# A recurrent block with routed experts on one core: gates by exp, ln and sigmoid instead of reciprocals, an earlier first job, output weights loaded further ahead

## The chip, the core and the metric

The kernel runs on one core of one Trainium2 chip. The metric is the device time of one execution in microseconds (us), as a median over runs. PE is the matmul engine (TensorE), DVE the vector engine, ACT the scalar engine, POOL the GpSimd engine, and SP the queue that issues most DMA transfers.

## What is computed

The input is x of 8 sequences of 1024 tokens with 512 features in float32. It is normalised (xn), and then two branches run on xn.

```
# recurrent branch, 512 -> 3 x 1024 -> 1024 -> 512
hidden, forget_gate, input_gate = split(xn @ W1 + b1)
diff           = softplus(-forget_gate) - softplus(-input_gate)
log_coeffs     = -softplus(diff)        # coefficient of the old state: f/(f+i), f and i the sigmoids
log_val_coeffs = -softplus(-diff)       # coefficient of the new value: i/(f+i)
h = scan over the tokens of  coeff * h + val_coeff * g(hidden)     # done in logs in the reference
s = h @ W2 + b2
# feed-forward branch
shared = (silu(xn @ shared_gate_w) * (xn @ shared_up_w)) @ shared_down_w
e      = argmax(xn @ gate_w)            # one of 32 experts per token
routed = (silu(xs @ gate[e]) * (xs @ up[e])) @ down[e],  xs = xn * sigmoid(max logit)
out    = x + s * silu(shared + routed)
```

Here g(v) is v + 0.5 for v >= 0 and sigmoid(v) below. In the reference the gates are called f for forget and i for input. In the kernel, the tile that holds the forget branch ends as the weight of the new value, and the tile that holds the input branch ends as the coefficient of the old state: with u_f and u_i the biased projections, sigmoid of (ln(1+exp(-u_f)) - ln(1+exp(-u_i))), negated or not, gives the two.

## The kernel before

**Stages.** The 8192 tokens are worked through in 16 chunks of 512 tokens (`NCHUNK`), features on the partitions. The first chunk is prepared at the top of the kernel (statistics, normalisation, PE transposes into `xnT`), the others while the chunk ahead of them is computed. After the chunks come the dispatch of tokens to experts, and then the 32 experts with a fixed number of tokens each, and a loop for tokens that were left over.

**Slots.** The order of all instructions in the chunk stage is written out by hand. Time is counted in slots. A chunk has 20 jobs (`JC`) of 7 slots, so 140 slots (`SC`). A job is one weight block of 512 x 256 (`natural`, tiles called `nat`): kinds f, i and h of the recurrence and g and u of the shared feed-forward, each in four pairs of 128 features. `at(slot, step)` puts a step into a slot, and the main loop first emits the matmuls of the slot with their evictions, then the slot's steps, and then as many matmuls of the output projection as are `due`. Every engine works in the order in which its instructions were emitted.

**Chunk 0** uses `plain`: per job 2 blocks of 4 matmuls of 512 columns, one per slot and two in the seventh. Each block has a PSUM bank of its own from `ps_b` (three banks), and ACT evicts it, with the bias where there is one. In the same chunk `combine` forms for each job the four weight sums S (`sums`), which `save` stores to DRAM for the later chunks: S0 and S3 on POOL, S1 and S2 on DVE.

**Chunks 1 to 15** use `multiply`: a 2 x 2 block scheme with seven half-sized products P1 to P7 instead of eight, each two matmuls of 256 columns, in the order P1, P4 (of two jobs back), P5, P7 (of one job back), P2, P6, P3. P1, P6, P7 and P4 accumulate in one bank (`b`), P5 and P3 in another (`c`), P2 in `a`; between two products of a bank ACT copies what stands in it, and DVE or POOL adds the parts one slot later (`join`). P3 is 4 slots after P5, the others in a bank are 5 slots apart. The sums of the moving operand, `t_sum`, are made on DVE at slots -5, -2, 3 and 8 of the chunk.

**Gates.** `Cell` works on one pair, 128 x 1024 elements. Its slots count from the first slot of the pair's f job. Before, with m = min(f, i, 0): POOL forms m - f and m - i (`less`), ACT takes exp of m, f and i, POOL adds m to f and i (`weigh`), DVE adds f and i (`total`), takes two reciprocals of 128 x 512 (`invert`) and multiplies both by them (`divide`). ACT's sigmoid and relu of h, two DVE steps (`value`, `weighed`) and two scans end the cell. Two tiles, tags `m` and `d`, are shared by all cells, one buffer each.

**Output projection.** `project_out` multiplies the recurrence's h by W2 and the shared hidden layer by its down weights, with the same seven products in units of one chunk and one of the two halves. A product is 8 matmuls (16 in the trace), and takes one weight block of 0.5 MB (`wP`), from the weights or from sums stored in `tdram`. `out_fetch` issues the next load whenever a product ends, into three buffers. The last two units run alone after the last job, while the experts' first weights (2 MB each, `e_wg`, `e_wu`, `e_wd`) are loaded on the same SP queue.

**Dispatch.** `Dispatch.ranks`, `places` and `slots` are generators that run one step per slot near the end of the chunks. A `yield` is a pause of one slot. `places` forms `terms` on DVE, pauses, and multiplies them on PE. Then 64 `enter` steps on POOL write token numbers into tables, `collect` and `merge` join these, and the experts' tokens are gathered.

In the trace every matmul stands as two records (two passes).

Of the kernel before, what the change touches and what calls it, by code (L numbers as in the profile page):

```python
# [8 lines left out]
FP = mybir.dt.float32  # L9
I32 = mybir.dt.int32  # L10
AF = mybir.ActivationFunctionType
ALU = mybir.AluOpType
# [21 lines left out]
def tile_kernel(  # L34
# [621 lines left out]
    for n in range(NJOB):  # L656
        if n >= 3:
            at(7 * (n - 2) + 2, load, n)
        if n >= JC:
            at(7 * (n - 2) + 4, fetch, n)  # L660
        else:
            for q, s in ((0, 0), (1, 2), (2, 3), (3, 4)):
                at(7 * n + s, combine, n, q)
            at(7 * n + 10, save, n)

# [32 lines left out]
    def plain(n, s):  # L698

        kind = JOBS[n % JC][1]  # L700
        for m in (s, s + 1) if s == 6 else (s,):
            block, k = divmod(m, KH)
            if k == 0:
                banks[n, block] = ps_b.tile([P, 512], FP, tag="b", name=f"b{block}_{n}")
            ps = banks[n, block]
            nc.tensor.matmul(  # L706
                ps, lhsT=natural[n][:, k, block * P : (block + 1) * P], rhs=xnTs[0][:, k, :],
                start=(k == 0), stop=(k == KH - 1),
            )
            if k == KH - 1:  # L710
                o = outs[n] if block else out_of(n)
                if kind in "gu":
                    nc.scalar.copy(o[:, block, :], ps)
                else:
                    nc.scalar.activation(o[:, block, :], ps, AF.Identity, bias=bias(n, block))

    def multiply(name, n):

# [77 lines left out]
    class Cell:  # L796
# [8 lines left out]
        def low(self):  # L805
            n = JC * self.c + JOBS.index((self.p, "f"))
            self.f, self.i, self.h = (outs[n + q] for q in range(3))

            self.m = self.tmp("m")
            nc.vector.scalar_tensor_tensor(self.m, self.f, 0.0, self.i, ALU.min, ALU.min)  # L810

        def less(self, v):
            v = getattr(self, v)
            nc.gpsimd.tensor_tensor(v, self.m, v, ALU.subtract)  # L814

        def exp(self, v):
            v = getattr(self, v)
            nc.scalar.activation(v, v, AF.Exp)

        def weigh(self, v):  # L820

            v = getattr(self, v)
            nc.gpsimd.tensor_tensor(v, self.m, v, ALU.add)  # L823

        def total(self):
            self.d = self.tmp("d")
            nc.vector.tensor_tensor(self.d, self.i, self.f, ALU.add)

        def invert(self, s):
            nc.vector.reciprocal(self.d[:, s, :], self.d[:, s, :])  # L830

        def divide(self, v):
            v = getattr(self, v)
            nc.vector.tensor_tensor(v, v, self.d, ALU.mult)

        def sigmoid(self):
            self.e = self.tmp("m")
# [25 lines left out]
        def plan(self):  # L863
            g = SC * self.c + 7 * JOBS.index((self.p, "f"))
            for slot, what, *args in (
                (24, self.low), (25, self.less, "f"), (25, self.less, "i"),
                (27, self.exp, "m"), (29, self.exp, "f"), (31, self.exp, "i"),
                (32, self.weigh, "f"), (33, self.weigh, "i"), (37, self.total),
                (38, self.invert, 0), (39, self.sigmoid), (40, self.positive),
                (41, self.invert, 1), (43, self.value), (44, self.weighed),  # L870
                (45, self.divide, "f"), (46, self.divide, "i"),
                (47, self.scan, 0), (48, self.scan, 1),
            ):
                at(g + slot, what, *args)

# [73 lines left out]

    units = [(c, half) for c in range(NCHUNK) for half in range(2)]  # L950
    out_w, out_s = {}, {}
    out_next = iter([(u, name) for u in units for name in UNIT])

    def out_fetch():

        u, name = next(out_next, (None, None))
        if u is None:
            return
        half = u[1]
        o = out_w[u, name] = out_tile(f"w{name}_{half}")  # L960
        if name in ("P1", "P2", "P3"):
            k, m = {"P1": (0, 0), "P2": (1, 0), "P3": (1, 1)}[name]
            nc.sync.dma_start(out=o, in_=out_block(half, k, m))
        else:
            q = {"P5": 1, "P6": 2, "P7": 3, "P4": 4}[name]
            nc.sync.dma_start(out=o.rearrange("p q f -> p (q f)"), in_=tdram[half, q][:, :])
# [97 lines left out]
    class Dispatch:  # L1064
# [69 lines left out]
        def places(self):  # L1134
# [42 lines left out]
                    terms[:, q * E : (q + 1) * E], of, by[:E, 0:1], None, ALU.mult  # L1177
                )
            nc.vector.tensor_copy(terms[:, 4 * E :], extra)
            for _ in range(4):  # L1180
                yield
            ps = work("terms")
            nc.tensor.matmul(
# [136 lines left out]
    for t in range(NT):  # L1320
        first.stats(t)
        first.variance(t, 1)
        first.spread(t, 1)
        if t:
            first.normal(t - 1)
            first.transpose(t - 1)
    first.normal(NT - 1)
    first.transpose(NT - 1)
    vps = work("vps")
# [71 lines left out]
    for now in range(END):  # L1401
# [153 lines left out]
```

## Time and profile before

| | us |
|---|---|
| median of 3 runs | 4299.56 (4299.24 to 4302.12) |
| profiled execution | 4299.96 |
| its span, first to last instruction | 4298.2 |
| PE busy | 4221.4 (98%) |
| DVE busy | 2830.7 (66%) |
| POOL busy | 1751.5 (41%) |
| ACT busy | 1607.1 (37%) |
| reciprocals (L830), 128 of 3.34 us on DVE | 427.9 |
| activation table loads in the gates, 127 of 1.28 us | 162.9 |

The page gives busy time per engine over the span, the groups of instructions by line with what ended the idle time before them, and the chain that ended last. The trace answers the same for any stretch of time. A wait is written as "engine, what it was to do, its line <- engine, what released it, its line", with the total in us, how often, and the longest. L706 is a matmul of chunk 0, L746 one of `multiply`, L1033 one of the output projection; L713 and L715 are the evictions in chunk 0, L760 and L762 those of `multiply`; L810 to L856 are the steps of `Cell`; L678 is `t_sum`, L488 a transpose of the preparation, L519 the router, L1183 the matmul of `terms`.

### The profile page before, as it was taken

Reading aid. Unit: us, or ns where it says so; the run is one execution under the profiler, and the core shown is the slowest. Engines: PE = TensorE matmul, PEld = TensorE weight load, DVE = VectorE, ACT = ScalarE, POOL = GpSimd, SP = SyncE. Lnnn points to the kernel's source line nnn. Section 1 sums busy time; section 2 is a strip of 40 time slices with the busy share of each in tenths; the row PEclk is TensorE's granted clock in tenths of the full one; section 3 lists DMA queues with packets and bytes.
Section 4 is the critical chain, followed back from the end, with each engine's and each line's share of the span. In section 5 each row is a group of like instructions: output and inputs, shape, how many; then the busy total and the mean of one; then the engine's idle time right before and its main releaser. Section 6 shows DMA issues by size and latency. Waiting matters only on the chain.

```text
span 4298.2 us, 52089 instructions
## 1 busy us (share of the span) xinstructions
PE 4221.4 (98%) x18703; PEld 3534.2 (82%) x18703; DVE 2830.7 (66%) x3637; ACT 1607.1 (37%) x3193; POOL 1751.5 (41%) x1410
## 2 busy tenths in 40 slices
PE   8899999999999999999999999999999999999998
PEld 3488888888888888888888888866777788889998
DVE  6786876887878768888787698823444444544444
ACT  3355555555555555555555554501111111111110
POOL 4444444543444445434444444741333233233221
PEclk9999999999999999999999999999999999999999
DMA  7567666666666666766666664575566657677773
GB/s 247 202 217 225 203 222 206 216 220 220 210 216 207 221 209 210 225 216 210 218 211 222 209 206 152 157 263 186 205 224 234 228 205 252 219 253 247 241 266 112
DMA packets 507240, 925.63 MB, mean 215 GB/s; under 512 B 38397, under 2 KB 325021, under 8 KB 498786
## 3 DMA queue, kind: packets, MB, share of 16 engines
q1 hardware_dynamic: 479394, 832.27, 58.7%
q0 software_dynamic: 27584, 89.98, 6.3%
q8 instruction: 150, 2.46, 0.2%
q14 instruction: 112, 0.92, 0.1%
HBM read 805.27 MB, written 134.92 MB: 219 GB/s over the span
## 4 chain that ended last, share of the span: by engine, by line
PE 91%; DVE 4%; POOL 2%; issue 2%; DMA 1%; ACT 0%; SPq 0%; POOLq 0%; DVEq 0%; ACTq 0%
PE b L746 23%; PE u L1033 17%; PE c L746 11%; PE e_g L272 11%; PE e_u L272 11%; PE acc L261 11%; PE a L746 6%; DVE d L830 1%; POOL i L814 0%; PE b L706 0%; DMA wP<-tdram 0%; PE lgp L519 0%; POOL tab L1280 0%; POOL i L823 0%; POOL f L823 0%
## 5 line engine op out<-in xcount | busy, mean ns | idle before, releaser
L746 PE MATMUL b<-t,sums 128*128 128x256 f32 x2400 | 619.2, 381 | 8.5 <-DVE t L678 6.3
L1033 PE MATMUL u<-wP,s 128*128 128x256 f32 x2048 | 600.8, 380 | 2.7 <-DMA wP<-tdram 2.7
L272 PE MATMUL e_g<-e_xsT,e_wg 128*128 128x296 f32 (+15 forms) x2048 | 518.3, 396 | 1.0 <-DVE e_xsT L243 1.0
L272 PE MATMUL e_u<-e_xsT,e_wu 128*128 128x296 f32 (+15 forms) x2048 | 518.2, 396 | 0.0
L746 PEld LDWEIGHTS b<-t,sums 128*128 128x128 f32 x2400 | 455.0, 191 | 74.4 <-issue 6.5
L261 PE MATMUL acc<-e_h,e_wd 128*128 128x296 f32 (+15 forms) x2048 | 513.0, 396 | 0.0
L272 PEld LDWEIGHTS e_g<-e_xsT,e_wg 128*128 128x128 f32 x2048 | 389.7, 190 | 87.5 <-DVE e_xsT L243 1.2
L261 PEld LDWEIGHTS acc<-e_h,e_wd 128*128 128x128 f32 x2048 | 389.8, 190 | 86.3
L272 PEld LDWEIGHTS e_u<-e_xsT,e_wu 128*128 128x128 f32 x2048 | 389.8, 190 | 86.4
L277 ACT ACTIVATE e_sig<-e_g 128x280 f32<-128x280 f32 (+15 forms) x256 | 101.9, 398 | 935.5 <-PE e_g L272 930.7
L1033 PEld LDWEIGHTS u<-wP,s 128*128 128x128 f32 x2048 | 390.2, 191 | 57.0 <-issue 5.0
L279 DVE TENSOR_TENSOR e_sig<-e_sig,e_g 128x280 f32<-128x280 f32 (+15 forms) x256 | 113.2, 442 | 481.9 <-ACT e_sig L277 481.5
L830 DVE RECIPROCAL d<-d 128x512 f32<-128x512 f32 x128 | 427.9, 3344 | 1.6
L359 POOL DMA_INDIRECT out_dram<-e_rest,idx x84 | 93.4, 1112 | 804.1 <-DVE e_rest L358 801.0
L213 POOL DMA_INDIRECT e_xs<-rec,fours x276 | 262.0, 949 | 180.9 <-DMA e_rest<-rec,idx 80.9
L814 POOL TENSOR_TENSOR f<-m,f 128x1024 f32<-128x1024 f32 x64 | 154.7, 2418 | 410.6 <-DVE m L810 321.8
L746 PE MATMUL c<-t,sums 128*128 128x256 f32 x1200 | 309.2, 380 | 6.4 <-DVE t L678 6.4
L746 PE MATMUL c<-xnT,sums 128*128 128x256 f32 x1200 | 310.3, 381 | 0.3
L746 PE MATMUL a<-xnT,nat 128*128 128x256 f32 x1200 | 309.9, 381 | 0.0
L746 PE MATMUL b<-xnT,nat 128*128 128x256 f32 x1200 | 308.1, 379 | 0.0
L746 PE MATMUL b<-t,nat 128*128 128x256 f32 x1200 | 308.1, 379 | 0.0
L280 DVE TENSOR_TENSOR e_h<-e_sig,e_u 128x280 f32<-128x280 f32 (+15 forms) x256 | 113.2, 442 | 245.7 <-PE e_u L272 245.4
(241 smaller groups left out, 7370.6 us busy)
## 6 DMA issues: line engine op xcount, KB each, us to landing
sums<-sdram SPq DMA_DIRECT2D x300, 512.0 KB, 4.8
nat<-in_L_attn_W_dram SPq DMA_DIRECT2D x192, 512.0 KB, 4.4
wP<-tdram SPq DMA_DIRECT2D x128, 512.0 KB, 4.3
e_wg<-L_ffn_routed_gate_w_dram SPq DMA_DIRECT2D x32, 2048.0 KB, 8.5
e_wu<-n_L_ffn_routed_up_w_dram SPq DMA_DIRECT2D x32, 2048.0 KB, 11.6
e_wd<-L_ffn_routed_down_w_dram SPq DMA_DIRECT2D x32, 2048.0 KB, 19.3
nat<-L_ffn_shared_gate_w_dram SPq DMA_DIRECT2D x64, 512.0 KB, 4.6
nat<-n_L_ffn_shared_up_w_dram SPq DMA_DIRECT2D x64, 512.0 KB, 4.3
```

The source lines that it names most:

```text
L213: nc.gpsimd.indirect_dma_start(out=r[:, b, :], out_offset=None, in_=rec1.rearrange("n (a d) -> (n a) d", a=NA), in_offset=bass.IndirectOff ...
L261: nc.tensor.matmul(accs[m][:, :W], lhsT=wd[:, j, m * P : (m + 1) * P], rhs=h[:, :W], start=(j == 0), stop=(j == NI - 1),)
L272: nc.tensor.matmul(o[:, :W], lhsT=w[:, k, j * P : (j + 1) * P], rhs=xsT[:, k, :W], start=(k == 0), stop=(k == KH - 1),)
L277: nc.scalar.activation(sig[:, :W], g[:, :W], AF.Sigmoid)
L279: nc.vector.tensor_tensor(sig[:, :W], sig[:, :W], g[:, :W], ALU.mult)
L280: nc.vector.tensor_tensor(h[:, :W], sig[:, :W], u[:, :W], ALU.mult)
L359: nc.gpsimd.indirect_dma_start(out=of[:, :], out_offset=bass.IndirectOffsetOnAxis(ap=col[:n, :], axis=0), in_=z, in_offset=None, bounds_ch ...
L746: nc.tensor.matmul(ps, lhsT=lhs[:, k, :], rhs=rhs[:, k, :], start=(new and k == 0), stop=(k == KQ - 1),  skip_group_check=True,)
L814: nc.gpsimd.tensor_tensor(v, self.m, v, ALU.subtract)
L830: nc.vector.reciprocal(self.d[:, s, :], self.d[:, s, :])
L1033: nc.tensor.matmul(ps[:, q, :], lhsT=lhs[:, q * P : (q + 1) * P], rhs=w[:, p, :],  start=(q == 0 and p == 0 and name in ("P1", "P2", "P5") ...
```

## The change

- The gates are computed as sigmoid of d and of -d, where d is ln(1+exp(-|f|)) - min(f,0) less the same of i, up to its sign. ACT does Abs, Exp and Ln of f and of i and the two sigmoids; DVE does `difference`, `less` and `more`. POOL does nothing in the cell. The scans stand at slots 45 and 47 instead of 47 and 48.
- The first job's matmuls are split into two halves of 256 tokens. The first half is emitted after the transposes of tiles 0 and 1, ahead of those of tiles 2 and 3 (`first_half`).
- `combine` of the sums S stands at slots 0, 2, 4 and 7 of a job (in the order S0, S2, S1, S3) instead of 0, 2, 3 and 4 (S0, S1, S2, S3).
- After the last job two more buffers (`far`) are made for output weights and two loads are issued at once, ahead of the first expert's weights; from there on two of five loads go to `far`.
- `places` pauses 9 slots instead of 4 between `terms` and its matmul.

```diff
-            for q, s in ((0, 0), (1, 2), (2, 3), (3, 4)):
+            for q, s in ((0, 0), (2, 2), (1, 4), (3, 7)):
                 at(7 * n + s, combine, n, q)
...
-            if k == 0:
+            if k == 0 and n:
                 banks[n, block] = ps_b.tile([P, 512], FP, tag="b", name=f"b{block}_{n}")
             ps = banks[n, block]
+            part = slice(0 if n else HT, T)
             nc.tensor.matmul(
-                ps, lhsT=natural[n][:, k, block * P : (block + 1) * P], rhs=xnTs[0][:, k, :],
-                start=(k == 0), stop=(k == KH - 1),
+                ps[:, part], lhsT=natural[n][:, k, block * P : (block + 1) * P],
+                rhs=xnTs[0][:, k, part], start=(k == 0), stop=(k == KH - 1),
             )
...
+    def first_half():
+        for block in range(2):
+            ps = banks[0, block] = ps_b.tile([P, 512], FP, tag="b", name=f"b{block}_0")
+            for k in range(KH):
+                nc.tensor.matmul(
+                    ps[:, :HT], lhsT=natural[0][:, k, block * P : (block + 1) * P],
+                    rhs=xnTs[0][:, k, :HT], start=(k == 0), stop=(k == KH - 1),
+                )
...
-            self.m = self.tmp("m")
-            nc.vector.scalar_tensor_tensor(self.m, self.f, 0.0, self.i, ALU.min, ALU.min)
...
-            nc.gpsimd.tensor_tensor(v, self.m, v, ALU.subtract)
+            t = self.tmp(tag)
+            setattr(self, "l" + v, t)
+            nc.scalar.activation(t, getattr(self, v), AF.Abs)
...
-            nc.scalar.activation(v, v, AF.Exp)
...
-            nc.gpsimd.tensor_tensor(v, self.m, v, ALU.add)
...
-            nc.vector.tensor_tensor(self.d, self.i, self.f, ALU.add)
...
-            nc.vector.reciprocal(self.d[:, s, :], self.d[:, s, :])
...
-            nc.vector.tensor_tensor(v, v, self.d, ALU.mult)
+            nc.scalar.activation(v, v, AF.Exp, scale=-1.0)
...
+            nc.scalar.activation(v, v, AF.Ln, bias=ones[:, 0:1])
...
+            nc.vector.tensor_tensor(d, d, self.li, ALU.subtract)
...
+            nc.vector.scalar_tensor_tensor(d, self.i, 0.0, d, ALU.min, ALU.add)
...
+            nc.vector.scalar_tensor_tensor(d, self.f, 0.0, d, ALU.min, ALU.subtract)
...
+            nc.scalar.activation(getattr(self, v), self.d, AF.Sigmoid, scale=sign)
...
-                (24, self.low), (25, self.less, "f"), (25, self.less, "i"),
-                (27, self.exp, "m"), (29, self.exp, "f"), (31, self.exp, "i"),
-                (32, self.weigh, "f"), (33, self.weigh, "i"), (37, self.total),
-                (38, self.invert, 0), (39, self.sigmoid), (40, self.positive),
-                (41, self.invert, 1), (43, self.value), (44, self.weighed),
-                (45, self.divide, "f"), (46, self.divide, "i"),
-                (47, self.scan, 0), (48, self.scan, 1),
+                (24, self.size, "f", "d"), (25, self.exp, "lf"), (26, self.size, "i", "m"),
+                (28, self.exp, "li"), (29, self.log, "lf"), (31, self.log, "li"),
+                (32, self.difference), (33, self.less), (34, self.more),
+                (36, self.gate, "i", 1.0), (37, self.gate, "f", -1.0),
+                (39, self.sigmoid), (40, self.positive),
+                (42, self.value), (43, self.weighed), (45, self.scan, 0), (47, self.scan, 1),
...
-        o = out_w[u, name] = out_tile(f"w{name}_{half}")
+        if "far" in pools:
+            turn = next(far_turn)
+            if turn % 5 < 2:
+                o = pools["far"].tile([P, NP, HC], FP, tag="far", name=f"far{turn}")
+            else:
+                o = out_tile(f"w{name}_{half}")
+            out_w[u, name] = o
+        else:
+            o = out_w[u, name] = out_tile(f"w{name}_{half}")
...
-            for _ in range(4):
+            for _ in range(9):
                 yield
...
+        if t == 2:
+            first_half()
...
+    pools["far"] = c1.enter_context(tc.tile_pool(name="far", bufs=2, side="right"))
+    for _ in range(2):
+        out_fetch()
     chunks[0].weight("g")
```

More of the change, by code (lines that the diff above doesn't have):

```diff
@@ L803, in tmp, with size, log, difference @@
             return jp.tile([P, 2, T], FP, tag=tag, name=f"{tag}{self.c}_{self.p}", bufs=1)
-        def low(self):
+        def size(self, v, tag):
             n = JC * self.c + JOBS.index((self.p, "f"))
             self.f, self.i, self.h = (outs[n + q] for q in range(3))
-            self.m = self.tmp("m")
-            nc.vector.scalar_tensor_tensor(self.m, self.f, 0.0, self.i, ALU.min, ALU.min)
-        def less(self, v):
-            v = getattr(self, v)
-            nc.gpsimd.tensor_tensor(v, self.m, v, ALU.subtract)
+            t = self.tmp(tag)
+            setattr(self, "l" + v, t)
+            nc.scalar.activation(t, getattr(self, v), AF.Abs)
         def exp(self, v):
             v = getattr(self, v)
-            nc.scalar.activation(v, v, AF.Exp)
-        def weigh(self, v):
+            nc.scalar.activation(v, v, AF.Exp, scale=-1.0)
+        def log(self, v):
             v = getattr(self, v)
-            nc.gpsimd.tensor_tensor(v, self.m, v, ALU.add)
-        def total(self):
-            self.d = self.tmp("d")
-            nc.vector.tensor_tensor(self.d, self.i, self.f, ALU.add)
[L829 to L833, printed above, removed]
-            nc.vector.tensor_tensor(v, v, self.d, ALU.mult)
+            nc.scalar.activation(v, v, AF.Ln, bias=ones[:, 0:1])
+        def difference(self):
+            self.d = d = self.lf
+            nc.vector.tensor_tensor(d, d, self.li, ALU.subtract)
+        def less(self):
+            d = self.d
+            nc.vector.scalar_tensor_tensor(d, self.i, 0.0, d, ALU.min, ALU.add)
+        def more(self):
+            d = self.d
+            nc.vector.scalar_tensor_tensor(d, self.f, 0.0, d, ALU.min, ALU.subtract)
+        def gate(self, v, sign):
+            nc.scalar.activation(getattr(self, v), self.d, AF.Sigmoid, scale=sign)
         def sigmoid(self):
@@ L951, in tile_kernel @@
     out_w, out_s = {}, {}
+    far_turn = iter(range(2 * len(UNIT)))
     out_next = iter([(u, name) for u in units for name in UNIT])
```

## The prediction

> **What bounds the kernel now.** I read the busy shares first, then busy time by stage, then what PE waited for, then ACT's and DVE's timelines at those waits.
>
> ```profile
> PE 4221.4 (98%) x18703; PEld 3534.2 (82%) x18703; DVE 2830.7 (66%) x3637; ACT 1607.1 (37%) x3193; POOL 1751.5 (41%) x1410
> ```
>
> PE is idle for only 4298.2 - 4221.4 = 76.8 us. The change removes no matmul, so I need to know where these 76.8 us lie. By stage (the stretch in us, its length, then busy time and count of PE, PEld, DVE, ACT and POOL, PE's granted clock, DMA share, GB/s):
>
> ```profile
> 12.90:180.20 167.30, 151.42 (x349) 65.59 (x348) 120.44 (x171) 58.84 (x75) 88.60 (x69) 0.95 0.66 224
> 180.20:204.00 23.80, 14.87 (x57) 12.11 (x57) 21.82 (x30) 6.68 (x14) 4.23 (x4) 0.86 0.41 139
> 204.00:2440.00 2236.00, 2235.28 (x10379) 1949.56 (x10378) 1746.12 (x1909) 1201.73 (x2397) 1002.51 (x715) 1.00 0.67 216
> 2440.00:2660.00 220.00, 209.69 (x953) 180.98 (x952) 175.50 (x236) 107.33 (x216) 99.22 (x72) 0.98 0.58 183
> 2800.00:2850.00 50.00, 41.12 (x183) 34.93 (x183) 14.53 (x25) 4.68 (x8) 19.49 (x21) 0.97 0.89 310
> 2850.00:4277.80 1427.80, 1427.25 (x6144) 1168.52 (x6143) 620.10 (x1132) 151.47 (x340) 426.58 (x435) 1.00 0.65 224
> ```
>
> From 204 to 2440 us PE misses 0.7 us: the 13 chunks there cannot get faster, though most of the reciprocals run in them. The expert stage from 2850 on is full and untouched. What can be won lies in chunk 0 and its end, around the dispatch table, and at the hand-over to the experts. PE's waits name the causes (total us, times, longest):
>
> ```profile
> PE b L706 <- ACT u L713: 10.7, 2, 5.7
> PE terms L1183 <- DVE terms L1179: 6.5, 1, 6.5
> PE c L746 <- DVE t L678: 6.4, 1, 6.4
> PE b L746 <- DVE t L678: 6.3, 3, 3.8
> PE u L1033 <- DMA wP<-L_ffn_shared_down_w_dram: 5.2, 1, 5.2
> PE lgp L519 <- DVE xnT L488: 3.7, 1, 3.7
> PE u L1033 <- DMA wP<-tdram: 2.7, 1, 2.7
> ```
>
> The first is an ACT eviction queued behind a gate exp that waits for POOL; the third is `t_sum` queued behind reciprocals (timelines of ACT and DVE: start, duration, operation, idle time before it):
>
> ```profile
> 78.58 1.06 ACT L818 ACTIVATE m<-m 128x1024 f32<-128x1024 f32 x1 [5.29 <-POOL i L814]
> 80.49 0.56 ACT L713 COPY u<-b 128x512 f32<-128x512 f32 x1
> ...
> 177.00 6.55 DVE L830 RECIPROCAL d<-d 128x512 f32<-128x512 f32 x2
> ...
> 185.89 0.68 DVE L678 TENSOR_TENSOR t<-xnT 128x512 f32<-128x512 f32 x1
> ```
>
> After each long wait the matmuls also run slow for some us. PE's timeline, with one pass of 512 columns at 0.427 us and of 256 at 0.215 us when full: 40 passes took 19.69 instead of 17.1 from 81.11, 50 took 24.37 instead of 21.35 from 124.72, 14 took 7.97 instead of 6.0 from 153.76, 12 took 5.8 instead of 2.6 from 186.62; small rest 0.4: **11 us** in chunk 0 and its end. Likewise 2.5 us after the wait at 2575, 1.7 at 2620, 1.9 at 2816.
>
> **What the Trainium skill says.** "TensorE: Matmul & The Clock Gate", What's actually happening: the clock halves after an idle window of about 3.4 us and returns after as long busy. The trace agrees (waits of 3.7 us and more are followed by slow passes; that of 1.59 us at 2702 is not). "ScalarE: Activation LUTs", What ACT_TABLE_LOAD costs: 1283 ns and a drain of about 1380 ns. The trace has 1283 ns, but no drain: a load ends at 852.44 and its exp starts at 852.45. I use 1.28. "SBUF — State Buffer", the shared port pair of DVE and POOL: a two-input DVE operation and a POOL one exclude each other; it fits L847, 1.22 us alone and 1.75 beside POOL.
>
> **The change, part by part.**
>
> *Gates, 64 cells.* Removed from DVE: L810 1.22, L827 1.26, two reciprocals 6.69, two L834 3.04 = 12.2; added: three at 1.22 = 3.7; saves 8.5 per cell. POOL loses 2.42 + 2.73 + 2.41 + 2.45 = 10.0 per cell. An Abs, an Ln and a scaled Exp or Sigmoid stand in no row; I price them at the rows of Exp, Sigmoid and Relu, 1.05 to 1.06 us (the same ScalarE section gives every function one rate), low end the same, high end 1.2 with the bias pointer of Ln. ACT gets eight activations for three and one more table load (the built kernel's ACT list has a load before exp, before ln and before sigmoid; Abs needs none): 5 x 1.06 + 1.28 = +6.6 us per cell; its share in the full chunks goes from 1202/2236 = 54% to about 69%. ACT gate work waits for POOL no more; the one cross-engine wait is gate i behind three DVE steps.
>
> Does PE feel ACT? The tightest use is P5 (slot phase 2) to P3 (phase 6, same bank): P5's eviction must end before P3's slot. A slot is 170.7/140 = 1.22 us (784 passes x 0.215 and the router). Back to back an activation costs 0.96 us and an eviction 0.36. From slot 24 (time 0): Abs, eviction, load and Exp, eviction, Abs end at 6.06; eviction, eviction, Exp 7.72; eviction, load, Ln 10.33; P5's eviction of slot 30 ends at 10.69, P3 of slot 34 starts at 12.2: **1.5 us spare**. The second Ln ends at 12.0; on DVE difference, less and more with 1 to 2.5 us of queued joins and preparation end at 16.7 to 18.2; gate i ends at 18.1 to 19.3, P5's eviction of slot 37 at 19.6 at worst, P3 of slot 41 starts at 20.7: **1.1 us spare**. An output eviction (0.58) fits into either. What queues on DVE behind `difference` are joins, whose parts have two buffers, and `t_sum`, 7 slots ahead. The kernel before already shows such lags without loss:
>
> ```profile
> 940.62 1.06 ACT L818 ACTIVATE m<-m 128x1024 f32<-128x1024 f32 x1 [3.20 <-POOL i L814]
> 941.59 0.35 ACT L760 COPY p<-b 128x256 f32<-128x256 f32 x1
> ```
>
> So I charge 3 us for new ACT waits; from 0 to 25 (0.4 per cell in 60 cells).
>
> *Chunk 0.* Idle 5.71 + 1.51 + 4.98 + 3.68 + 6.42 + 0.51 + 2.00 = 24.8, slow 11: 36 us. Every one of these waits has reciprocals or POOL's subtractions ahead of it. DVE needs 120 us of 167 there and loses some 30; POOL loses 40. ACT's burst there lags 3 to 4 us, its three 512-wide banks allow two blocks, 6.9 us. I take 33 back (20 to 36).
>
> *Sums S spread out.* Same four operations per job, 20 jobs. It breaks up POOL and DVE waiting for each other; `save` stays at slot 10 and the next `load` precedes it on SP, so SP is not held. Counted in chunk 0, else nothing; if that cover fails, a late `save` holds SP, and a weight has 12 slots before its use.
>
> *First job in halves.* 16 half passes go ahead of transposes 2 and 3: they start at 9.4 (ACT's copy) instead of 12.9. Full speed at about 13.8 leaves 1.25 us of them: 15.05; two transposes, their two ACT copies, vps 2.75; then 3.44: 21.2 against 12.9 + 4.4 + 4.66 = 22.0. Gain 0.7 (-0.6 if cold throughout, to 2.5).
>
> *Table.* Waits 6.5 + 3.8 + 1.6 + 1.7 (the last for the last cell's scan), slow 4.2: 17.8. DVE is without a gap from 2588 to 2620 and loses 8.5 us there, and `terms` gets 5 slots, 6 us. I take 14.5 (8 to 17.8). The 5 slots move `enter` on POOL, `collect` on SP, the merges on DVE and the gathers later, on POOL past nothing that PE needs sooner; they end about 11 slots before the last output matmul, so the cover stands.
>
> *Output weights ahead.* 7.9 us idle and 1.9 slow. In the built SP list the last seven 0.5 MB loads now precede the table's write and its eight re-reads, two of them e_wg's 2 MB; five instead of three are in flight, 17 us of PE work ahead instead of 10. No bytes are added. The two extra buffers lie where the jobs' tiles were: their triggers may hold SP, with e_wg behind them, until the last hidden product has been read, which is due one slot earlier. Late next: e_wd, issued some 17 us before its use (22 before), while the DMA window at 2820 moves 365 GB/s (2 MB in 5.5 us). I take 8 (0 to 9.8).
>
> **Sum:** 0.7 + 33 + 14.5 + 8 - 3 = 53.2; the profiled execution's 4299.96 (span 4298.2 and 1.8 around it; 0.4 over the median 4299.56) gives **4247 us**.
>
> **Rivals.**
> (a) *Gate i waits longer for DVE*, 0.4 us past the spare in 60 cells: 24 us, 4271. For: DVE is in order and carries preparation at the same slots; against: 31% of its gate work is left.
> (b) *Chunk 0 keeps half its loss* to transposes that wait for their DMA or sums for POOL: 4247 + 16 = 4263. For: lgp's wait is for a transpose whose data made a trip through DRAM; against: DVE was busy for 19.25 of the 20 us from 140 to 160.
> (c) *Slower: ACT sets the pace.* If a load costs the skill's 2.66, two loads put P5's first eviction at 13.45, past 12.2, and the gate's at 22.4, past 20.7: 1.6 us per cell at the least, x60 = 96 against 56 won: 4340. It decides from 0.9 us per cell. Against: the load's end in the trace.
> (d) *The waits stay*, because their true last releaser is another: 4299.
>
> **How the numbers follow.** Forecast 0.68 (own range 4236 to 4260), (a) 0.14, (b) 0.09, (c) 0.05, (d) 0.04. 0.2% is 8.6 us, about what can be told from no change. Faster 0.91, same 0.04, slower 0.05. Low 4236 is nearly all of 36 + 17.8 + 9.8 back; high 4275 takes in (a) and (b).
>
> **What would show it.** Right: PE idle falls to some 35 us, of which 6 are the start and 20 the end; no ACT u wait at L706; job-end `t_sum` wait gone; 204-to-2440 span's counterpart as full as before; DVE near 2285 busy, POOL 1110, ACT 2030. Wrong: many short waits of matmuls `c` for ACT copies of `c` (a, c), or a gap in table loads.

## The result, and the profile after

The changed kernel takes 4237.15 us (median of 4 runs, 4235.61 to 4237.33), the kernel before 4299.88 on the same chip (4299.24 to 4302.12): ratio 0.985, interval 0.9835 to 0.9869, so 62.7 us less. The profiled execution took 4237.12 with a span of 4235.3. The last eight kernels below (numbers 5 to 12) ran on two chips where the kernel before took 4319 us instead of 4300, so their times are not to be set beside those of the others. Four of them (5, 6, 11 and 12) have the changed kernel's code up to the last chunks; they reach the router of chunk 15 at 2461.6 to 2462.5 us, the changed kernel at 2462.8, and PE is full in all of them up to 2590 us. What is longer on those chips thus lies after 2590, and the eight are read, up to there, by the moment at which PE reaches the same matmul.

The page of the changed kernel, busy time by engine, and the head of its chain that ended last:

```profile
PE 4198.4 (99%) x18719; PEld 3527.1 (83%) x18719; DVE 2082.2 (49%) x3445; ACT 1980.4 (47%) x3577; POOL 1084.3 (26%) x1154
...
PE 99%; issue 0%; DMA 0%; DVE 0%; SPq 0%; ACT 0%; POOL 0%; POOLq 0%
```

PE is now idle for 4235.3 - 4198.4 = 36.9 us instead of 76.8. DVE lost 748 us of work and POOL 667; ACT gained 373 and stays under half. What PE still waits for (total us, times, longest):

```profile
PE tp L507 <- DVE x L469: 6.5, 2, 6.1
PE u L1052 <- issue: 6.1, 1, 6.1
PE b L722 <- DMA nat<-in_L_attn_W_dram: 1.8, 1, 1.8
PE e_g L272 <- DVE e_xsT L243: 1.0, 1, 1.0
```

Gone are the ACT evictions of chunk 0, `t_sum`, the transpose ahead of the router, the terms and both waits for output weights. The second line is a new wait, at the hand-over. The profile names no releaser for it, but the timelines of PE and DVE do:

```profile
2757.53 3.62 PE L1052 MATMUL u<-wP,s 128*128 128x256 f32 x16
2767.23 8.60 PE L1052 MATMUL u<-wP,s 128*128 128x256 f32 x32 [6.08 <-issue]
...
2766.44 0.69 DVE L1064 TENSOR_TENSOR o<-u,a 128x512 f32<-128x512 f32 x1 [8.63 <-DMA rec<-o]
```

P5 of the last unit needs the bank in which P2 stands. DVE adds P2 into the output tile, which it may do only when the store of that tile's last content (`rec<-o`) is done, and PE starts 0.10 us after DVE's step ends, at 2767.13. All 3584 passes of the output projection (32 units of 7 products of 16 passes) stand in the trace, some now reading `far` in place of `wP`, so the gap of 6.1 us is idle time. The expectations of numbers 4 and 5 rest on a gap of 2.6 us here, as if one product were missing from the trace; that is a misreading. By stage (stretch, length, then busy time and count of PE, PEld, DVE, ACT and POOL, PE's granted clock, DMA share, GB/s):

```profile
12.90:156.60 143.70, 142.35 (x365) 65.94 (x364) 84.78 (x172) 86.21 (x102) 44.17 (x53) 1.00 0.78 266
156.60:180.00 23.40, 23.40 (x109) 20.48 (x108) 16.72 (x29) 9.68 (x21) 3.95 (x5) 1.00 0.71 245
180.00:2370.00 2190.00, 2190.00 (x10195) 1912.97 (x10194) 1134.26 (x1715) 1483.57 (x2666) 456.68 (x500) 1.00 0.67 215
2370.00:2590.00 220.00, 220.00 (x1023) 191.38 (x1022) 128.72 (x244) 139.70 (x258) 50.06 (x54) 1.00 0.65 208
2737.00:2787.00 50.00, 42.94 (x194) 36.88 (x193) 15.03 (x25) 5.28 (x9) 20.26 (x22) 0.93 0.86 296
```

Chunk 0 (but for 1.35 us, two waits for ACT's copies of `xnT`), its end and the stretch of the dispatch table are full, at clock 1.00 where it was 0.95, 0.86 and 0.98. Only the hand-over to the experts is not: 7.1 us short, 6.1 of it this gap and 1.0 the wait for the first expert's tokens (`e_xsT`).

Three lengths on PE's timeline serve for every kernel here: to the router of chunk 2 (the start, chunk 0 and the first part of chunk 1), from there to the router of chunk 15 (13 full chunks), and on to the first transpose of the experts (table and hand-over).

| kernel | to router 2 | 13 full chunks | to the experts |
|---|---|---|---|
| before | 271.5 | 2232.3 | 341.5 |
| changed | 236.7 | 2226.1 | 319.8 |
| gates alone | 236.6 | 2226.2 | 320.5 |
| all but the gates | 266.1 | 2232.6 | 331.3 |
| without the half job | 235.8 | 2226.2 | 321.5 |
| without `far` | 235.5 | 2226.1 | 322.2 |
| reciprocals short | 250.6 | 2226.2 | (other chip) |
| POOL short | 247.1 | 2226.2 | (other chip) |
| one more ACT step | 236.2 | 2241.7 | (other chip) |
| three more ACT steps | 246.7 | 2379.7 | (other chip) |

So the change won 34.8 + 6.2 + 21.7 = 62.7 us. The last term splits at the last product of the chunks: up to there it is 288.9 us before and 269.4 after (19.5 won), from there to the experts 52.6 and 50.3 (2.3 won). The 269.4 is the same in numbers 1, 3 and 4. The 50.3 is not firm: number 3, whose code is the same there, takes 52.1.

The middle term was not to be expected from PE's busy time, which looked full before. It shows in the weight loads. Rows by form of the kernel before, 204 to 2440 us (busy, mean ns, idle before and its releaser):

```profile
L746 PEld LDWEIGHTS b<-t,sums 128*128 128x128 f32 x2080 | 393.6, 190 | 55.9 <-ACT p L760 4.4
L746 PEld LDWEIGHTS c<-xnT,sums 128*128 128x128 f32 x1042 | 197.1, 190 | 31.6 <-ACT p L760 5.5
```

The same rows of the changed kernel, 180 to 2370 us:

```profile
L756 PEld LDWEIGHTS b<-t,sums 128*128 128x128 f32 x2046 | 387.7, 190 | 52.2
L756 PEld LDWEIGHTS c<-xnT,sums 128*128 128x128 f32 x1020 | 193.8, 190 | 26.3
```

Before, two or three times a chunk, P3 (`c<-xnT,sums`), P6 or P7 (`b<-t,sums`) started 0.1 to 0.3 us late, because ACT, queued behind a gate step that waited for POOL, had not yet copied the product ahead of it. Summed over the starts of the passes this is 6.1 us. These pauses are so short that PE's modelled ends cover them, and the busy time of PE shows nothing.

How the new burst fits on ACT is seen in its timeline in one cell (start, duration, line, operation; a gap would stand in brackets):

```profile
817.19 1.09 ACT L826 ACTIVATE m<-m 128x1024 f32<-128x1024 f32 x1
818.15 0.49 ACT L772 ACTIVATE h<-b,vec 128x256 f32<-128x256 f32 x1
818.65 1.28 ACT L830 ACT_TABLE_LOAD   x1
819.95 1.15 ACT L830 ACTIVATE d<-d,ones 128x1024 f32<-128x1024 f32 x1
821.00 0.35 ACT L770 COPY p<-c 128x256 f32<-128x256 f32 x1
```

and in PE's, P5 and then P3 of the same bank:

```profile
817.24 1.03 PE L756 MATMUL c<-t,sums 128*128 128x256 f32 x4
...
821.99 0.59 PE L756 MATMUL c<-xnT,sums 128*128 128x256 f32 x2
```

The eviction `p<-c` ends at 821.35 and P3 starts at 821.99: 0.6 us to spare. Over the 260 such evictions of the full chunks the least is 0.60; 26 have 0.65 or less, 39 have 0.89 or less, and the median is 3.26. Before, the least was 0.05 (13 of them), which is a wait. The load of the Ln table ends at 819.93 and the Ln starts at 819.95, so no drain stands here either ("ScalarE: Activation LUTs", What ACT_TABLE_LOAD costs, gives one of about 1380 ns; the measurement decides).

### The profile page after: what moved, and what is told of

Read it like the earlier page. It is cut to its first block, busy times and chain, and to the rows that moved or that the text cites. A ratio compares the mean times of both kernels' runs of the same rounds, so it can differ in the third digit from the quotient of the medians.

```text
span 4235.3 us, 51808 instructions
## 1 busy us (share of the span) xinstructions
PE 4198.4 (99%) x18719; PEld 3527.1 (83%) x18719; DVE 2082.2 (49%) x3445; ACT 1980.4 (47%) x3577; POOL 1084.3 (26%) x1154
## 4 chain that ended last, share of the span: by engine, by line
PE 99%; issue 0%; DMA 0%; DVE 0%; SPq 0%; ACT 0%; POOL 0%; POOLq 0%
PE b L756 24%; PE u L1052 18%; PE c L756 12%; PE e_g L272 11%; PE e_u L272 11%; PE acc L261 11%; PE a L756 6%; PE b L707 3%; PE lgp L519 0%; PE lgt L529 0%; DMA nat<-in_L_attn_W_dram 0%; PE b L722 0%; DMA e_rest<-rec,idx 0%; DMA out_dram<-e_rest,idx 0%; PE bef L1129 0%
## 5 line engine op out<-in xcount | busy, mean ns | idle before, releaser
L756 PEld LDWEIGHTS b<-xnT,nat 128*128 128x128 f32 x1200 | 228.0, 190 | 31.4 <-issue 0.5
L756 PEld LDWEIGHTS c<-t,sums 128*128 128x128 f32 x1200 | 228.0, 190 | 31.0
L756 PEld LDWEIGHTS a<-xnT,nat 128*128 128x128 f32 x1200 | 228.0, 190 | 31.0
```

Of the source, the lines that this page charges most:

```text
L756: nc.tensor.matmul(ps, lhsT=lhs[:, k, :], rhs=rhs[:, k, :], start=(new and k == 0), stop=(k == KQ - 1),  skip_group_check=True,)
```

## The experiments

**Theory:** the gates alone carry the gain, by taking DVE and POOL out of the way of ACT's evictions, of `t_sum` and of the terms; the other edits matter at the start and the hand-over. **Rivals:** the spread sums carry chunk 0; the pause carries the table; or the new burst on ACT has room, and then again it has none.

**1. The gates alone.** The kernel before with the changed `Cell`, nothing else.

```diff
 # before.py
-class Cell: low, less, exp, weigh, total, invert, divide, ...
+class Cell: size, exp, log, difference, less, more, gate, ...
```

> The kernel before with the gate edit alone (Cell's steps and slots), nothing else of the change. Theory (the gates leaving DVE and POOL end the waits of chunk 0, the short waits of the full chunks and those around the table): 36 us from chunk 0, 5.7 from the full chunks, 13 to 17 from the table stage, nothing at the hand-over: about 4242, 4238 to 4248. Rival (the sums' spreading and the longer pause do a good part of it): 4255 or more, with PE waits left in chunk 0 or at terms.

Measured: 4237.69 us (4236.57 to 4238.82) against 4299.78, ratio 0.9855 (0.9838 to 0.9871), the whole gain. PE's waits that are left at the end are those for output weights:

```profile
PE u L1033 <- DMA wP<-L_ffn_shared_down_w_dram: 4.3, 1, 4.3
PE u L1033 <- DMA wP<-tdram: 1.3, 1, 1.3
```

There is none at the terms, though this kernel pauses only 4 slots: DVE reaches them early once the reciprocals are gone. And none in chunk 0, though the sums S stand where they stood.

**2. All but the gates.** The changed kernel with the old `Cell`.

```diff
-class Cell: size, exp, log, difference, less, more, gate, ...
+class Cell: low, less, exp, weigh, total, invert, divide, ...
```

> The changed kernel with the gates of before: first job in halves, sums spread, far weights and the longer pause stay. Theory: chunk 0 keeps its waits; 0.9 lost by the first half, up to 9 won at terms, about 5 at the hand-over: 4285 to 4294. Rival (sums spread relieves DVE in chunk 0): 4275 or less, with the waits for ACT u and for t_sum in chunk 0 at half or less.

Measured: 4284.52 us (4284.07 to 4284.81), ratio 0.9964 (0.995 to 0.9978): 15.3 us less than before. 5.4 of it come by router 2, from the half job or the spread sums, which no run tells apart in the old kernel. 10.2 come after router 15, 9.4 of these ahead of the last product of the chunks, where the longer pause does its work: the wait at the terms falls from 6.5 to 0.5 us. What PE waits for in chunk 0 is the old list:

```profile
PE b L707 <- ACT u L714: 6.5, 2, 3.8
PE b L756 <- DVE t L678: 6.1, 3, 2.9
PE lgp L519 <- DVE xnT L488: 4.6, 1, 4.6
```

So the parts do not add: 62.1 alone and 15.3 alone make 62.7 together. The other edits are worth 15 us in the old kernel and half a microsecond behind the new gates, which remove the same waits; half a microsecond is less than the runs of one kernel differ.

**3. Without the half job.**

```diff
-            part = slice(0 if n else HT, T)
+            part = slice(0, T)
...
-        if t == 2:
-            first_half()
```

> The changed kernel with the first job whole, as before. Theory (the half waits for its weights' DMA, runs at the slow clock and puts the transposes behind it: 0.9 us lost at the first router transposes): 4236.2, and the job after the router's transposes starts at 25.4 instead of 26.4. Rival (the half brings the 0.7 us of the prediction): 4237.8 and a start at 27.

Measured: 4238.30 us (4236.96 to 4239.09), ratio 0.9856 (0.984 to 0.9872). PE reaches the first transposes of the router's logits at 25.1 us. Over all the kernels of this study the nine with the half job reach them at 24.1 to 25.9 (mean 24.9), the five without, the kernel before among them, at 24.9 to 25.9 (mean 25.2). A gain of 0.3 is not told apart from the scatter of the first loads, for which the half job now waits itself: the 1.8 us at L722 above. To router 2 this kernel is even 0.9 ahead of the changed one, and over the whole 1.2 behind; what the half job is worth, and whether it is a gain, stays open.

**4. Without `far`.**

```diff
-    pools["far"] = c1.enter_context(tc.tile_pool(name="far", bufs=2, side="right"))
-    for _ in range(2):
-        out_fetch()
```

> The changed kernel without the two extra output-weight buffers and without the two early loads. Theory (they took 5.5 of the 9.8 us at the hand-over): 4242 to 4243, with PE waits for wP of some 5 to 8 us back. Rival (with the table's chain later the early loads are hidden anyway, what is lost there is the wait for an output store): 4236 to 4238, the wait of PE behind DVE's o as long as in the changed kernel.

Measured: 4239.29 us (4238.01 to 4239.96), ratio 0.9859 (0.9843 to 0.9876). The two waits for weights are back:

```profile
PE u L1052 <- DMA wP<-tdram: 4.5, 1, 4.5
PE u L1052 <- DMA wP<-L_ffn_shared_down_w_dram: 1.9, 1, 1.9
```

They are 6.4 us together, and the gap of 6.1 us behind `rec<-o` is gone: in the changed kernel the loads further ahead trade one wait for the other. By the times they are worth some 2 us (4239.29 less 4237.15). The stretch to the experts is 322.2 instead of 319.8, but number 3 needs 321.5 with the changed kernel's code, so one profile doesn't tell 2 us here. Nor does it tell what the longer pause costs: the kernel with the gates alone, which has neither `far` nor the long pause, needs 320.5, 1.7 less than this one.

**5. What holds the hand-over: the last unit's outputs in other buffers.** In the changed kernel SP's timeline at the hand-over is

```profile
2742.58 0.38 SPq L193 DMA_DIRECT2D e_wg<-L_ffn_routed_gate_w_dram  x1
2743.91 0.34 SPq L985 DMA_DIRECT2D wP<-tdram  x1
2744.30 10.89 SPq L1310 DMA_DIRECT2D two<-tab  x8
2755.28 0.38 SPq L985 DMA_DIRECT2D wP<-tdram  x1
2755.85 0.34 SPq L193 DMA_DIRECT2D e_wu<-n_L_ffn_routed_up_w_dram  x1
2756.29 0.38 SPq L1025 DMA_DIRECT2D rec<-o  x1
```

SP stands for 10.89 us at the table's reads, held by transfers ahead of them (4.5 us by that of `e_wg`, 1.9 by `far`, 0.9 by `wP`), and the output's store `rec<-o` goes out only then. Its tile is the one that the last unit writes, and DVE waits for it, with PE behind:

```profile
DVE o L1064 <- DMA rec<-o: 8.6, 1, 8.6
```

The experiment gives the last unit's outputs tiles of their own.

```diff
-            o = [op.tile([P, 2, H], FP, tag=f"o{m}", name=f"o{half}_{c}_{m}") for m in range(2)]
+            if n == len(units) - 1:
+                o = [hp.tile([P, 2, H], FP, tag="r", name=f"o{half}_{c}_{m}", bufs=5) for m in range(2)]
+            else:
+                o = [op.tile([P, 2, H], FP, tag=f"o{m}", name=f"o{half}_{c}_{m}") for m in range(2)]
```

> The changed kernel with the last output unit's o tiles in two buffers that the recurrence no longer needs, so that DVE need not wait for the store of the unit before. Theory (what is left at the hand-over, 2.6 us of wait and 1.7 of slow passes, hangs on that store, which SP issues late behind the table's loads): 4233 to 4234, DVE's wait for rec<-o gone. Rival (the weights' transfers would have stopped PE at the same place): 4236 to 4238, with a wait for wP or far in its stead.

Measured: 4264.79 us (4264.04 to 4268.37), ratio 0.9878 (0.9861 to 0.9894). DVE's wait for `rec<-o` is gone. PE, which stood 6.1 us behind it, now stops nearly as long at the next thing that SP sent late:

```profile
PE u L1055 <- DMA wP<-tdram: 5.8, 1, 5.8
```

From the last product of the chunks to the first transpose of the experts it takes 50.0 us, in the changed kernel 50.3. So the store alone did not set the end of the hand-over; it and the weights both go out only after SP's stand at the table's reads, which number 11 shortens.

**6. The pause back at 4 slots.**

```diff
-            for _ in range(9):
+            for _ in range(4):
                 yield
```

> The changed kernel with a pause of 4 slots before the matmul of terms, as before. Theory (with DVE relieved the longer pause is not needed, terms are formed 7 us ahead; it only pushes the table's loads behind the far loads on SP and so delays the output store): no wait at terms, 4234 to 4236. Rival (terms is late without it): a wait of 1 to 6 us at terms, 4238 to 4244.

Measured: 4279.85 us (4272.21 to 4283.85), ratio 0.9905 (0.9887 to 0.9923). PE does not wait at the terms, which it reaches at 2533.9 instead of 2540.5, so the pause is not needed there. The whole is 15 us longer than number 5 on the same chip, in the stretches after 2590 us: in the two stretches of 50 us from there PE is idle for 5.3 and 11.7 us, in number 5 for 2.8 and 5.4, and in the changed kernel on its own chip for none. Its four runs lie 11.6 us apart. Why, the runs don't say; what the pause costs or brings here is left open.

**7. Reciprocals short.** The kernel before with a short DVE step in place of each reciprocal (the weights are not formed).

```diff
-            nc.vector.reciprocal(self.d[:, s, :], self.d[:, s, :])
+            nc.vector.tensor_scalar(
+                self.d[:, s, :], self.d[:, s, :], 0.0, 0.25, ALU.mult, ALU.add
+            )
```

> The kernel before with a tensor_scalar (to a constant) of about 0.6 us in place of each reciprocal of 3.34 us; the gates are then wrong, POOL's four steps stay. Theory (DVE's queue carries most of the loss): the waits for t_sum, xnT and terms go with their slow passes (about 28 us) and a good part of ACT's waits in chunk 0, the short waits of P3 for ACT stay (6 us): 4250 to 4262. Rival (POOL's subtractions carry it): 4275 or more.

**8. POOL short.** The kernel before with POOL's four gate steps on 128 of 1024 columns.

```diff
-            nc.gpsimd.tensor_tensor(v, self.m, v, ALU.subtract)
+            nc.gpsimd.tensor_tensor(v[:, :, :64], self.m[:, :, :64], v[:, :, :64], ALU.subtract)
...
-            nc.gpsimd.tensor_tensor(v, self.m, v, ALU.add)
+            nc.gpsimd.tensor_tensor(v[:, :, :64], self.m[:, :, :64], v[:, :, :64], ALU.add)
```

> The kernel before with POOL's four gate steps on 128 of 1024 columns each, the gates then wrong, and the reciprocals as they are. Theory (DVE's queue carries most of the loss): the short waits of P3 in the full chunks go (6 us), chunk 0 loses part of its ACT waits, DVE gains some us by the shared port: 4272 to 4284, and the waits for t_sum and terms stay. Rival (POOL carries it): 4262 or less.

Measured: 4280.75 us (4275.03 to 4282.34), ratio 0.9913 (0.9897 to 0.993), for number 7, and 4272.60 (4270.44 to 4275.85), 0.9894 (0.9878 to 0.9911), for number 8. By router 15 the full change is 41.0 us ahead of the kernel before (2503.8 - 2462.8); shorter reciprocals alone bring 27.0 of them (2476.8), shorter POOL steps alone 30.5 (2473.3). Together that is more than there is: neither engine is the cause by itself. In the kernel before, ACT's exp of m waited 95.2 us for POOL, POOL's first subtraction 321.8 for DVE, and DVE's sum 35.6 for POOL, with the reciprocals behind it; a break at either place frees most of the loss. That DVE carries the most, my theory for these two, fell. In both the small pauses of the full chunks are gone as well (2226.2); I had expected that number 7 keeps them. Number 7 still waits 2.6 us at the terms, number 8 does not, which has its reason in POOL (last section).

The two engines also slow each other. One join, `u<-c,u` of 128x256, by form over the full chunks, in the kernel before:

```profile
L772 DVE TENSOR_TENSOR u<-c,u 128x256 f32<-128x256 f32 x52 | 47.7, 918 | 21.8 <-ACT c L760 21.8
```

and with POOL's steps short:

```profile
L772 DVE TENSOR_TENSOR u<-c,u 128x256 f32<-128x256 f32 x52 | 24.7, 476 | 46.7 <-ACT c L760 46.7
```

With the reciprocals short, and POOL's steps whole, it was 1245 ns.

**9 and 10. How tight ACT is.** The changed kernel with one, and with three, more Abs on `li`, in place, ahead of the Ln; the values stay.

```diff
+            if v == "lf":
+                for _ in range(1):        # 3 in number 10
+                    nc.scalar.activation(self.li, self.li, AF.Abs)
             nc.scalar.activation(v, v, AF.Ln, bias=ones[:, 0:1])
```

> The changed kernel with one more step in every cell's burst on ScalarE: |li| in place, ahead of the two gates' Ln (the values stay what they are; 64 more instructions of 1024 columns, about 0.96 us each by the row of i<-li, 1048 ns less the overlap at its ends). It measures how tight the burst is. Theory (the spare measured in the changed kernel's trace, between the end of P5's eviction and P3's start: 0.60 us at the least, 0.89 at the tenth part of 260 evictions): about 26 evictions overrun by 0.1 to 0.36 us each, so +5 to +8 us: 4242 to 4246 us, and small waits of PE for ACT at P3 come back. Rival (the spare of the prediction, 1.5 us at the router phases and 1.1 at the others): nothing is late, 4237 us.

> The same with three such steps in every cell's burst, 2.9 us more. Theory: the evictions that stand right behind the burst, about one for each of the 52 cells in full chunks, overrun by 1.5 to 2.3 us, and the cells of chunk 0 by about as much as the chain there takes the ACT steps, so +80 to +120 us: 4317 to 4357 us, with PE's waits for ACT at L760 the first row. Rival (ACT's queue has slack and the passes between absorb it, since ACT is busy only 47% of the span): under +20 us, below 4257.

Measured: 4286.94 us (4283.83 to 4292.08), ratio 0.9928 (0.9913 to 0.9943), and 4459.18 (4450.36 to 4461.46), 1.0326 (1.031 to 1.0342). Up to router 15, where the chips agree, the full chunks are 15.6 us longer with one step, 153.6 with three. PE's waits from 180 to 2370 us with one step:

```profile
PE c L756 <- ACT p L770: 5.5, 25, 0.2
```

those of its weight loads there:

```profile
PEld c L756 <- ACT p L770: 20.2, 38, 0.6
```

and PE's waits with three:

```profile
PE c L756 <- ACT p L770: 105.9, 48, 2.4
```

In both the wait is P3 for the eviction of P5, at the place where the spare of 0.6 us was read. Both are larger than I expected, by a factor of two to three with one step and by 1.3 at the upper end with three. More evictions are late than the 26 that I counted: 38 waits stand in the loads of weights, which fits the 39 evictions with 0.89 us to spare or less. Three steps cost 153.6/52 = 2.95 us in each of the 52 cells, about what they last back to back, since after some of the waits the passes are slow as well (clock 0.99 over that stretch, 1.00 before). The rival with 1.5 us of room, and that with slack to absorb it, both fall. With the three steps the kernel is slower than the one before. An engine that is busy for 47% of the span, and for 68% of the full chunks (1483.57 of 2190 us), is thus, at 39 places in 52 cells, 0.60 to 0.89 us from making PE wait.

**11 and 12. A better hand-over.** The first expert's gate weights are asked for 14 turns later, behind the table's reads; number 12 has the pause at 4 as well.

```diff
-    chunks[0].weight("g")
     k = 0
...
-        if k in (6, 26):
-            chunks[0].weight("ud"[k // 26])
+        if k in (14, 20, 26):
+            chunks[0].weight({14: "g", 20: "u", 26: "d"}[k])
```

> The changed kernel with the first expert's gate weights (e_wg) asked for 14 turns later, behind the table's reads and the fetch of the last unit's sums, where it stood ahead of them on SP's queue. Theory (at the hand-over SP was held 10.9 us at the reads of the table, 4.5 us of it by the transfer of e_wg, and so asked for rec<-o and the last weights late): DVE's wait for rec<-o shrinks by about 4 us and PE with it: 4232 to 4235 us. Rival 1 (the other transfers ahead hold SP as long): 4237. Rival 2 (e_wg now comes late and the first expert waits for it): over 4238, with a wait for e_wg at L272.

> The same with the pause ahead of the terms' product back at 4 turns. Theory (no kernel with the new gates waited at the terms, with 9 turns or 4, so the pause only delays the dispatch by five turns, about 1.7 us by the tails of the kernel with the gates alone and of the one without early weights): 1 to 2 us less than with 9 turns, 4230 to 4234 us. Rival (DVE reaches the terms later than PE in this order): a wait of PE at L1202 of 1 us or more and no gain.

Measured: 4255.55 us (4250.20 to 4260.11), ratio 0.9849 (0.9836 to 0.9863), for number 11, and 4267.62 (4266.20 to 4268.77), 0.9882 (0.9867 to 0.9897), for number 12. The stretch from the last product of the chunks to the first transpose of the experts, in the changed kernel (columns as in the table of stages above):

```profile
2732.30:2782.60 50.30, 44.22 (x199) 38.43 (x198) 14.59 (x21) 6.02 (x10) 20.73 (x22) 0.93 0.80 273
```

and in number 11:

```profile
2746.50:2789.00 42.50, 42.50 (x198) 37.41 (x198) 12.25 (x18) 6.02 (x10) 17.43 (x18) 1.00 0.84 292
```

42.5 us instead of 50.3: the hand-over is full at clock 1.00, and the 7.8 us are the gap of 6.1 and the 1.7 of slow passes behind it. SP stands at the reads for 6.30 us instead of 10.89. (The edit also takes 2 MB of traffic out of the time of the reads; the runs don't part this from the order on the queue.) More than half is given back at once, at a wait that follows:

```profile
2791.87 0.41 DVE L1333 TENSOR_SCALAR fours<-number,piece 128x372 int32<-128x372 f32 x1 [18.00 <-DMA number<-table]
...
2793.91 1.84 DVE L243 COPY e_xsT<-e_tp 128x512 f32<-128x512 f32 x3
```

DVE stands 18.0 us for rows of the table (8.8 in the changed kernel), with the copy of the expert's first tokens behind it, and PE waits 5.2 for that. To the experts' first product it is 49.3 us against 52.9, so 3.6 won, as far as one profile tells. On the same chip number 12 does the stretch in 43.8 and needs 46.4 to the first product, and loses more elsewhere after 2590 us; what was said of number 6 holds for it too. Neither was timed beside the changed kernel. The nearest is number 5, which does the hand-over as the changed kernel does: 4264.79 with a kernel before of 4319.3 there, against 4255.55 with 4319.8 for number 11. That points to the later gate weights as the better version; it is an inference over two chips and not a comparison.

## Why the prediction was right

The time was 10 us under the forecast of 4247, and 1 us inside the lower edge of its range, 4236 to 4260. By its steps:

- **What bounds, chunk 0** (0.7 + 33 predicted, 34.8 measured to router 2): right in place and size. The waits went that were named. The reason was half right: the prediction has reciprocals or POOL's subtractions ahead of every wait, and numbers 7 and 8 show a ring of the two, in which either alone brings some two thirds. It needed neither the spread sums (number 1) nor, as far as can be told, the half job (number 3), to which 0.7 was put.
- **"The 13 chunks there cannot get faster"**, with "I charge 3 us for new ACT waits" behind it: this is the step that failed, in sign. The full chunks gained 6.2 us where 3 were charged. The step was read from PE's busy time, while the groups by form of the same trace had PE's weight loads of `b<-t,sums` and `c<-xnT,sums` wait 5.2 and 6.3 us for ACT. No new wait for ACT came. 9.2 of the 9.5 us between the sum of 53.2 and the measured 62.7 are this; the misses of the other terms, +1.1, +5.0 and -5.7, nearly cancel.
- **Spare on ACT**: 1.5 us at P5 was predicted; the least measured is 0.60. The Ln with its bias pointer takes 1.15 and not 1.06, and evictions of other products stand in the burst. No wait came of it, so rival (a) did not happen, but numbers 9 and 10 show how near it was.
- **Table and hand-over** (14.5 + 8 predicted, 21.7 measured): right as a sum, and by luck, since the parts miss in opposite directions. Up to the last product of the chunks 19.5 were won, more than the range of 8 to 17.8. All of the 17.8 that the prediction counted went, and with it about 1 us of pauses as short as those of the full chunks (by the starts of PE's passes), which it had not counted. The 5 slots of pause were not needed for it (numbers 1 and 6). The hand-over gave 2.3 of 8. The waits for weights went as predicted; the wait behind `rec<-o`, 6.1 us and 1.7 of slow passes (32 passes took 8.60 us instead of 6.9), came in their place. "Late next: e_wd" was wrong: the store and the last weights were late, behind SP's stand of 10.89 us at the table's reads.
- **Busy times**: POOL 1110 predicted, 1084 measured; ACT 2030 and 1980; DVE near 2285 and 2082. DVE's miss of 203 us is work that was not removed but got shorter, with POOL's steps gone. By form over the whole kernels, the sums `s<-s,sh` of 128x256 went from 1146 to 518 ns, the joins `u<-c,u` from 911 to 480, and the two scans of 128x512 from 1649 and 1616 to 1315 and 1272.
- **Rivals.** (b) and (d) are excluded by the waits that went. (c) is excluded by the load's end in the trace; its point of decision, 0.9 us too late in each cell, lies between numbers 9 and 10: the first is late by 15.6/52 = 0.30 per cell and still faster than the kernel before, the second by 2.95 and slower.

## What to carry to other kernels

A stage in which PE is busy for all of its time may still lose a tenth of a microsecond at many places: read the idle column of the weight loads as well before calling it full. When work is moved to an engine with idle time, its share of the span says little; what counts is the time between the product it must copy and the next one that needs the bank, and that can be found by adding known steps until PE waits. A load that is moved ahead can trade one wait for another of the same length, as `far` did. And edits that remove the same wait are to be tried one by one: here one of five carried all but half a microsecond.

## What the runs showed of the hardware

- A small DVE step can take ten times its time beside POOL. `terms` from a 32x32 tile, 223 ns where POOL is free (number 8), took 2.30 us in the kernel before, and ended when POOL's addition did, at 2580.75. DVE's timeline in the kernel before:

```profile
2578.48 2.30 DVE L1176 TENSOR_SCALAR terms<-ident,pos 32x32 f32<-32x32 f32 x1
```

  and POOL's, of the same kernel:

```profile
2578.23 2.52 POOL L823 TENSOR_TENSOR i<-m,i 128x1024 f32<-128x1024 f32 x1
```

  This fits what the Trainium skill says in "SBUF — State Buffer", Who interferes with whom: DVE in a mode that uses two ports and POOL share a pair of ports, which the one that issues first holds for its whole instruction while the other stands. POOL's step started 0.25 us ahead here. The trace doesn't show the mode of the DVE step. The delay is 2 of the 6.5 us that PE waited for the terms.
- Waits of about 2 us can slow PE as well. With three more ACT steps, in PE's timeline of one cell:

```profile
1006.49 2.07 PE L756 MATMUL c<-xnT,sums 128*128 128x256 f32 x4 [2.42 <-ACT p L770]
1008.36 1.06 PE L1055 MATMUL u<-wP,s 128*128 128x256 f32 x2
...
1010.28 0.59 PE L1055 MATMUL u<-wP,s 128*128 128x256 f32 x2
```

  After a wait of 2.42 us four passes took 2.07 us instead of the 1.03 of a full pace, and two 1.06 instead of 0.59; from 1010.28 on the pace is back. The granted clock is 0.50 from 1006.2 to 1009.6 us. Not every such wait does it: from 180 to 2370 us the clock fell to half 14 times, each time beside one of 48 waits of 1.89 to 2.42 us. "TensorE: Matmul & The Clock Gate" (What's actually happening) gives an idle window of about 3.4 us for this; here a wait of 2.4 sufficed.
- An activation with a bias pointer to a column of ones (Ln, 128x1024) takes 1148 to 1154 ns, the same size without one 1048 to 1078, in the changed kernel.
- Three table loads per cell, 192 in all, take 1283 ns each; after 160 of them the next step of ACT starts within 20 ns.
